# Expert weights of the second mixture: through a DRAM tensor and GpSimd in place of TensorE and VectorE

## The chip, the cores and the metric

The kernel runs on one core of a Trainium2 chip. The metric is the device time of one execution in microseconds, as the median of several runs. All work on the engines is in fp32. The profile names the engines PE (TensorE; PEld is its loading of weights), DVE (VectorE), ACT (ScalarE), POOL (GpSimd) and SP (SyncE, which here issues nearly all transfers).

## The reference, cut to what matters

Four layers follow one another on 64 sequences of 128 tokens with 128 features, each with a layer norm ahead of it and a residual sum behind it: cross-attention, a mixture of 8 gated experts (2 per token), a second cross-attention, and a second mixture. The change lies in the second mixture and in the preparation of the second attention, which runs at the same time.

```python
def _L1_xattn_ref(queries, keys, values, ...):      # keys = values = ctx: 120 rows, 16 heads of 8
    scores = jnp.einsum('bhqd,bhkd->bhqk', Q, K) / jnp.sqrt(d)
    attn = jax.nn.softmax(scores, axis=-1)
    out = jnp.einsum('bhqk,bhkd->bhqd', attn, V)
    return out @ W_o.T + b_o

def _L1_ffn_ref(x, Wg, bg, W1, W2):                 # E = 8, K = 2, R = 64, SCALING = 2
    logits = xf @ Wg.T + bg
    top_gates, top_idx = jax.lax.top_k(logits, K)
    top_gates = jax.nn.softmax(top_gates, axis=-1)
    h = jax.nn.gelu(jnp.einsum('nd,erd->enr', xf, W1), approximate=False)
    eout = SCALING * jnp.einsum('enr,edr->ned', h, W2)
    sel = jnp.take_along_axis(eout, top_idx[:, :, None], axis=1)
    out = jnp.sum(top_gates[:, :, None] * sel, axis=1)

x = x + _L1_xattn_ref(_layernorm(x), ctx, ctx, ...)
x = x + _L1_ffn_ref(_layernorm(x), ...)
```

The kernel computes the second mixture densely: the hidden rows of all 8 experts (8 x 64 = 512) are made for every token, each row is multiplied by the weight that its expert has for the token (zero for the six that were not chosen), and one product over all 512 rows gives the output. These weights are called shares or gates below.

## The kernel before, in words

The 64 sequences are worked on in 16 groups of four (GB = 4, NG = 16). The residual stream of each group stays in on-chip memory (`x_0` to `x_15`). The first attention, with the routing of the first mixture beside it, fills the first 620 us of the profiled execution, the tiles of the first mixture's experts follow, and the second attention with the second mixture beside it begins at about 955 us.

The order of the instructions on PE, DVE, ACT and POOL is the order in which the program writes them (`manual_schedule`). On SP a planner sets the order, by when it expects a transfer's inputs to be there. Each engine works through its queue in order, so an instruction that waits holds all that stand behind it.

`attention(1, ...)` is a loop over `it` from 0 to 68. Iteration `it` works on several sequences at different stages: the row maxima of the scores of sequence `it` (L407 on PE, L414 on DVE), the shift of sequence `it-1` by its maxima (L459 on PE, L462 on DVE, into the queries that the next iteration's scores read), scores and exponentials of `it-2` (L430 on PE, L438 on ACT), values of `it-3` (L475 on PE, L484 on ACT), and the output of `it-3` to `it-5` (L491 to L516). Eight PSUM banks are handed out in turn by `mtile()`.

With j = `it % 4`, `prep(it, half)` makes ready the next group of four, in two halves per iteration:

- j = 0: nothing.
- j = 1: the keys (L202 on PE, L207 on ACT), then `prep_heads`: four copies of the keys on DVE, each masked to a part of the heads (L313). The copies are first read by L407 in the next group's j = 0.
- j = 2: the values (L214 on PE, L221 on DVE), then the transposed normed input (L176 on PE, L177 on ACT).
- j = 3: the queries (L292 on PE, L295 and L301 on ACT).

Beside the attention runs `Aside1`. Once per iteration, after values and scores and ahead of the first half of `prep`, `piece` takes one step of the generator `experts()`. A group has four steps, and the first falls on j = 2:

1. j = 2: the gates of the group are transposed on PE (L1417) and copied by ACT into `gT` (L1419): row 32 j + e holds expert e's share for the 128 tokens of sequence j. Four products with `lw1` (L1424) give the hidden rows of two experts each for all 512 tokens, and ACT applies Gelu (L1427) into `h1`, chunk by chunk.
2. j = 3: 16 products of `gT` with the constant `select` (L1434; fp32 products take two instructions each) spread the shares over the partitions of their experts, into four PSUM banks, and DVE multiplies `h1` by them (L1439).
3. j = 0: the output product of two sequences over the four chunks (L1445), and its sum into the residual stream (L1450).
4. j = 1: the same for the other two, and the transfer of the group's result to memory (L1452).

`h1` and `gT` have one buffer each. In the same iterations POOL gathers the rows of the first mixture for later sequences (L1364), adds them to the residual stream (L1376), after which DVE takes the statistics of the sum (L112, L113), and makes the normed rows (L155 to L167, L526). `self.router.call` advances the routing of the second mixture (small instructions between L681 and L778, L1402, L1403), two calls per iteration.

The first group's experts begin in iteration 18 and those of the group numbered 12 in iteration 66. When the loop ends, four groups of the mixture are not finished, and `rest` takes the remaining steps of `experts()` one after the other, with three router calls after each.

A transfer in this kernel is one `dma_start` on SP, and its pieces are spread over the core's DMA engines.

## Time and profile before

| What | Value |
|---|---|
| median of 3 runs | 1576.28 us (1573.33 to 1578.66) |
| the profiled execution | 1516.1 us |
| its span, from the first to the last instruction | 1514.3 us |
| mean granted clock of TensorE | 0.989 |
| busy: PE, DVE, ACT, POOL | 94%, 73%, 56%, 42% of the span |
| first and last start of L1417 (gates transposed) | 1070.5 and 1500.4 us |
| L1417 of group 12, the last one inside the loop | 1461.4 us |
| L1417 of groups 13, 14 and 15 | 1479.6, 1491.1 and 1500.4 us |
| POOL busy from 1160 to 1190 us | 18.3 of 30 us |
| DMA share and rate from 1160 to 1190 us | 0.13, 36 GB/s |

The durations in the text below come from this one profiled execution. A group row of the profile gives the engine, the operation, the tile written and the tiles read, the shapes, the number of instructions, then the busy time in all, the mean of one in ns, and the idle time of the engine just ahead of such instructions with what ended it. The chain is followed back from the last instruction to what released each, and is shown in order of time (start, length, what). A timeline row has start, length, engine, line, and in brackets the idle time ahead. A clock of 1.00 is TensorE's full speed.

### The profile page before, as it was taken

Reading aid. Unit: us, or ns where it says so; the run is one execution under the profiler, and the core shown is the slowest. Engines: PE = TensorE matmul, PEld = TensorE weight load, DVE = VectorE, ACT = ScalarE, POOL = GpSimd, SP = SyncE. Lnnn points to the kernel's source line nnn. Section 1 sums busy time; section 2 is a strip of 40 time slices with the busy share of each in tenths; the row PEclk is TensorE's granted clock in tenths of the full one; section 3 lists DMA queues with packets and bytes.
Section 4 is the critical chain, followed back from the end, with each engine's and each line's share of the span. In section 5 each row is a group of like instructions: output and inputs, shape, how many; then the busy total and the mean of one; then the engine's idle time right before and its main releaser. Section 6 shows DMA issues by size and latency. Waiting matters only on the chain.

```text
span 1514.3 us, 42033 instructions
## 1 busy us (share of the span) xinstructions
PE 1421.0 (94%) x16620; PEld 1107.5 (73%) x16620; DVE 1102.4 (73%) x3024; ACT 847.6 (56%) x1740; POOL 640.4 (42%) x1195
## 2 busy tenths in 40 slices
PE   7999999999999999888999999898999999999987
PEld 5777777777777677777888888566666776767665
DVE  6777888888888988455754444687777778787763
ACT  4666666666666666543333333566667566666643
POOL 4123254646465635654001122377546555454210
PEclk9999999999999999999999999899999999999999
DMA  8433333333222221366766667111011111100000
GB/s 201 120 80 80 79 82 96 89 93 94 63 66 60 58 73 40 107 184 202 214 197 199 201 195 205 49 34 34 22 36 29 39 35 32 31 29 23 8 16 22
DMA packets 143719, 133.03 MB, mean 88 GB/s; under 512 B 48546, under 2 KB 126114, under 8 KB 141602
## 3 DMA queue, kind: packets, MB, share of 16 engines
q1 hardware_dynamic: 135330, 113.02, 27.3%
q0 software_dynamic: 8192, 17.32, 3.7%
q8 instruction: 132, 2.16, 0.6%
q14 instruction: 65, 0.53, 0.1%
HBM read 97.32 MB, written 32.97 MB: 86 GB/s over the span
## 4 chain that ended last, share of the span: by engine, by line
PE 69%; DVE 15%; DMA 4%; POOL 4%; ACT 4%; issue 2%; SPq 1%; POOLq 0%; DVEq 0%; ACTq 0%
PE bank L430 11%; PE bank L394 10%; PE bank L475 9%; PE bank L1115 9%; PE bank L1424 4%; PE bank L1445 4%; DVE nm L414 4%; PE bank L1128 3%; DMA q<-xs 2%; PE bank L407 2%; PE bank L214 2%; DVE q L462 2%; PE bank L511 2%; PE bank L681 2%; PE bank L202 2%
## 5 line engine op out<-in xcount | busy, mean ns | idle before, releaser
L414 DVE TENSOR_REDUCE nm<-bank 128x2 f32<-128x496 f32 (+1 forms) x768 | 463.5, 662 | 77.6 <-PE bank L430 61.8
L438 ACT ACTIVATE p<-bank 120x512 f32<-120x512 f32 (+1 forms) x768 | 402.1, 605 | 126.8 <-PE bank L430 123.9
L430 PE MATMUL bank<-q,k 32*120 32x256 f32 (+1 forms) x3072 | 438.1, 399 | 11.4 <-DVE nm L414 5.2
L430 PEld LDWEIGHTS bank<-q,k 32*120 32x120 f32 (+1 forms) x3072 | 293.5, 181 | 56.8 <-DVE nm L414 17.3
L394 PE MATMUL bank<-k,q 32*128 32x248 f32 x2048 | 291.0, 399 | 0.7 <-ACT q L334 0.5
L394 PEld LDWEIGHTS bank<-k,q 32*128 32x128 f32 x2048 | 202.2, 189 | 47.9 <-issue 11.0
L1120 DVE TENSOR_TENSOR p<-p,bank 128x256 f32<-128x256 f32 x213 | 88.0, 420 | 121.0 <-ACT p L1119 120.5
L475 PE MATMUL bank<-p,v 128*32 128x128 f32 (+1 forms) x4096 | 175.6, 275 | 0.2
L407 PE MATMUL bank<-k,qf 32*128 32x480 f32 x512 | 153.8, 602 | 0.8 <-ACT qf L295 0.8
L807 POOL DMA_INDIRECT xs<-xn,at x128 | 129.2, 1009 | 27.9 <-issue 24.3
L1119 ACT ACTIVATE p<-bank 128x256 f32<-128x256 f32 x213 | 81.0, 384 | 98.9 <-PE bank L1115 97.9
L484 ACT COPY ov<-bank 128x256 f32<-128x256 f32 x128 | 48.1, 376 | 143.5 <-PE bank L475 143.4
L475 PEld LDWEIGHTS bank<-p,v 128*32 128x32 f32 (+1 forms) x4096 | 108.8, 109 | 22.8 <-issue 13.7
L1364 POOL DMA_INDIRECT yb<-ys,back x112 | 108.5, 969 | 27.7 <-issue 19.5
L1115 PE MATMUL bank<-q 128*128 128x256 f32 x516 | 118.6, 379 | 1.6 <-ACT q L1106 1.6
L462 DVE SCALAR_TENSOR_TENSOR q<-bank,c_smask,q 128x256 f32<-128x256 f32 x256 | 111.1, 475 | 8.2 <-PE bank L459 7.8
L167 POOL TENSOR_SCALAR xn<-x,mv,rstd 128x128 f32<-128x128 f32 x252 | 110.2, 449 | 7.5 <-issue 1.4
L1115 PEld LDWEIGHTS bank<-q 128*128 128x128 f32 x516 | 94.7, 190 | 13.0 <-ACT q L1106 1.9
L475 PE MATMUL bank<-p,vc 120*32 120x128 f32 x2048 | 103.2, 272 | 0.0
L155 POOL TENSOR_SCALAR rstd<-mv 128x4 f32<-128x4 f32 x32 | 6.3, 198 | 219.9 <-DVE mv L113 123.0
L301 ACT ACTIVATE q<-bank,c_a_bq,c_hmask 128x512 f32<-128x512 f32 x124 | 90.1, 789 | 9.8 <-PE bank L292 9.8
L1157 POOL DMA_INDIRECT kvT<-ys,back x16 | 15.4, 961 | 189.7 <-DMA vc<-xs 114.0
(224 smaller groups left out, 2465.7 us busy)
## 6 DMA issues: line engine op xcount, KB each, us to landing
q<-in_w SPq DMA_DIRECT2D x43, 576.0 KB
vc<-in_w SPq DMA_DIRECT2D x28, 576.0 KB
vc<-in_ctx_v SPq DMA_DIRECT2D x16, 960.0 KB
ys<-zero SPq DMA_DIRECT2D x71, 128.0 KB
k<-in_ctx_k SPq DMA_DIRECT2D x32, 240.0 KB
q<-xs SPq DMA_DIRECT2D x43, 128.0 KB
ys<-q SPq DMA_DIRECT2D x43, 128.0 KB
x<-in_x SPq DMA_DIRECT2D x16, 256.0 KB
```

Source lines behind the costliest of these rows:

```text
L167: nc.gpsimd.tensor_scalar(xn[:, j, :D], xg[g][:, j, :], self.mv[:, b, 0:1], self.rstd[:, b : b + 1], ALU.add, ALU.mult,)
L301: nc.scalar.activation(q4s[g][:, :, s, :], pq.rearrange("p (b q) -> p b q", b=GB), AF.Identity, bias=w["bq"][:, s : s + 1], scale=hmask[:, ...
L394: nc.tensor.matmul(pa[:, u, :], lhsT=q4s[g][r, j, s, :], rhs=k2[g % 2][r, s // 2, j, :], start=True, stop=True,)
L407: lambda: nc.tensor.matmul(pa, lhsT=qfs[g][r, j, :], rhs=k4s[g][r, :, j, :], start=True, stop=True),
L414: nc.vector.tensor_reduce(nm[b % 2].rearrange("q i (a s) -> q a i s", s=16)[:, 2 * ra + v : 2 * ra + v + len(slots) // 2, :, 0], pa.rearra ...
L430: nc.tensor.matmul(pb[:n, v * 256 : (v + 1) * 256], lhsT=k2[g % 2][r, v, j, k0 : k0 + n], rhs=q4s[g][r, j, 2 * v : 2 * v + 2, :].rearrange ...
L438: nc.scalar.activation(ps_[b][:n, c, ra, :], pb[:n], AF.Exp, scale=SCALE)
L462: nc.vector.scalar_tensor_tensor(q, pm, smask[:, v : v + 1], q, ALU.mult, ALU.add)
L475: nc.tensor.matmul(pav[32 * ra : 32 * ra + 32, v * S : (v + 1) * S], lhsT=vs[g % 2][c][:, j, 4 * v + ra, i, :], rhs=p[:n, c, ra, (2 * v + ...
L807: s = nc.gpsimd.indirect_dma_start(xs, bass.IndirectOffsetOnAxis(at[:, j, k : k + 1], 0), xn, None)
L1115: nc.tensor.matmul(ph[:, u, :], lhsT=w[:, c, u * 128 : (u + 1) * 128], rhs=xT, start=True, stop=True)
L1364: nc.gpsimd.indirect_dma_start(y[:, k, b % 2, :], None, ys, bass.IndirectOffsetOnAxis(back[:, b, k : k + 1], 0),)
```

## The change

- The shares no longer go over PE. `gT` becomes a part of a larger tile `share` (128 x 4 x 512, 8 KB on each partition, one buffer). Four transfers write its rows, 8 x 128 each, to a DRAM tensor of 16 KB (two of these are used in turn). Two further transfers read it back, each into 64 partitions and with the same rows for all of them, in pieces of 2 KB: 1 MB a group in all. `select` and the 16 products are gone.
- The multiplication of `h1` by the shares moves from DVE (L1439, four instructions by sequence) to POOL (four by chunk). Its step comes two iterations after the hidden layer: an empty step stands between.
- Both output products and both sums are one step, in the iteration after the multiplication. A group has four steps as before: hidden layer in j = 2, nothing in j = 3, multiplication in j = 0, output in j = 1.
- After the Gelu of a group ACT carries out one Exp on a single element (`again`).
- `prep_heads` moves from the second half of j = 1 to j = 2, ahead of the values. This concerns the groups from the third on.

On SP the planner puts the four writes of a group after the copy of its gates, then the load of a later group's context (`kvT`), then the two reads, then the output.

```diff
                     elif g < NG:
                         pieces = (
-                            (), (lambda: prep_k(g), lambda: prep_heads(g)),
-                            (lambda: prep_v(g), lambda: prep_x(g)),
+                            (), (lambda: prep_k(g),),
+                            (lambda: (prep_heads(g), prep_v(g)), lambda: prep_x(g)),
                             (lambda: prep_q(g, 0), lambda: prep_q(g, 1)),
                         )[j]
...
     ys = hbm.tile([NTL * TT, D], F32, name="ys", tag="ys")
+    shares_ = [hbm.tile([E, GB, S], F32, name=f"shares_{k}", tag=f"shares_{k}") for k in range(2)]
...
-    select = load_const("select", [128, 4, 128], a["select"])
+    again = const.tile([1, 2], F32, name="again", tag="again")
+    nc.vector.memset(again, 0.0)
...
                 nc.tensor.transpose(pt, gates.rearrange("p b e -> p (b e)"), ident)
-                gT = self.pool.tile([128, S], F32, name="gT", tag="gT", bufs=1)
+                share = self.pool.tile([128, 4, GB * S], F32, name="share", tag="share", bufs=1)
+                gT = share[:, 3, :S]
                 nc.scalar.copy(gT, pt)
+
+                there = shares_[g % 2]
+                for j in range(GB):
+                    nc.sync.dma_start(there[:, j, :], gT[32 * j : 32 * j + E, :])
+                for i in range(2):
+                    nc.sync.dma_start(
+                        share[64 * i : 64 * i + 64],
+                        there.rearrange("(c i) j t -> i c (j t)", i=2)[i]
+                        .unsqueeze(0).to_broadcast([64, 4, GB * S]),
+                    )
                 xnT = self.xnTs.pop(g)
                 hT = self.pool.tile([128, 4, GB * S], F32, name="h1", tag="h1", bufs=1)
                 for c in range(4):
...
                     nc.scalar.activation(hT[:, c, :], ph, AF.Gelu)
+
+                nc.scalar.activation(again[:, 1:2], again[:, 0:1], AF.Exp)
                 yield
 
-                pg = [self.mtile().rearrange("p (c t) -> p c t", c=4) for _ in range(GB)]
+                yield
                 for c in range(4):
-                    for j in range(GB):
-                        r = slice(32 * j, 32 * j + 32)
-                        nc.tensor.matmul(
-                            pg[j][:, c, :], lhsT=select[r, c, :], rhs=gT[r, :], start=True, stop=True
-                        )
-                for j in range(GB):
-                    h = hT[:, :, j * S : (j + 1) * S]
-                    nc.vector.tensor_tensor(h, h, pg[j], ALU.mult)
+                    nc.gpsimd.tensor_tensor(
+                        hT[:, c, :], hT[:, c, :], share[:, c, :], ALU.mult
+                    )
                 yield
                 for j0 in range(0, GB, 2):
...
                             out[g * GB : (g + 1) * GB].rearrange("b p d -> p b d"), xg[g]
                         )
-                    yield
+                yield
```

The host no longer makes `select`.

More of the change, by code (lines that the diff above doesn't have):

```diff
@@ L1534, in _laid_out @@
     o["steps256"] = np.arange(CAP // TT, dtype=np.float32) * TT
-    t = np.zeros((4, 32, 4, 2, 64), np.float32)
-    for e in range(E):
-        t[:, e, e // 2, e % 2, :] = 1.0
-    o["select"] = t.reshape(128, 4, 128)
     o["tiles"] = np.arange(NA, dtype=np.float32).reshape(1, -1)
```

## The prediction

> **What bounds the kernel now.** I read the busy shares first, then the chain of work that ended last, the groups of instructions of the stretch the change touches (1066 us to the end), its timeline engine by engine, and the clock of the last 40 us. Every touched line runs after 1066 us, except the removed load of `select` at the start.
>
> ```profile
> PE 1421.0 (94%) x16620; PEld 1107.5 (73%) x16620; DVE 1102.4 (73%) x3024; ACT 847.6 (56%) x1740; POOL 640.4 (42%) x1195
> ```
> PE looks like the bound. In the stage itself the chain shows a mixture: PE in the heavy iterations, DVE and a table load in the light ones.
>
> ```profile
> 1311.33 1.28 ACT L438
> 1313.27 1.02 PE bank L1434 x24
> 1314.34 2.48 DVE h L1439 x4
> ...
> 1320.87 2.07 PE bank L1445 x16
> ...
> 1331.78 1.52 DVE k L313 x4
> ...
> 1495.97 0.70 DVE h L1439
> 1496.71 3.84 PE bank L1445 x32
> 1500.66 3.44 PE bank L1424 x8
> ```
> The first five lines lie in the loop: the table load before the exponentials, the share products, DVE's multiplication and the scaled keys end a wait once per group. The last three lie behind the loop, where one group's experts follow the other with nothing beside them.
>
> The groups of the stage, and the one POOL instruction of the shape that is added (in columns: busy, mean ns | idle before):
>
> ```profile
> L1439 DVE TENSOR_TENSOR h<-h,bank 128x512 f32<-128x512 f32 x64 | 39.7, 682 | 22.4 <-PE bank L1434 22.3
> L1434 PE MATMUL bank<-gT,c_select 32*128 32x128 f32 x512 | 30.2, 288 | 5.6 <-ACT p L438 4.7
> L526 POOL TENSOR_TENSOR x<-x,c_a_bo 128x512 f32<-128x512 f32 x11 | 14.0, 1269 | 0.9
> ```
>
> Where cover lies in an iteration, from the timeline of one group (brackets: idle before the instruction, and what ended it):
>
> ```profile
> 1240.59 0.76 DVE L221 TENSOR_TENSOR v<-bank,c_a_bv 120x256 f32<-120x256 f32 x2 [3.54 <-PE bank L214]
> 1244.87 1.28 ACT L438 ACT_TABLE_LOAD   x1 [0.76 <-PE bank L430]
> 1259.64 0.20 POOL L155 TENSOR_SCALAR rstd<-mv 128x4 f32<-128x4 f32 x1 [7.11 <-DVE mv L113]
> ```
> DVE stands 3.54 us while PE makes the hidden layer; POOL stands 7.11 us; ACT loads the table only when the first exponential is due. The last line is for later, a load of 256 KB from the chain's start, with 0.43 us of issue before it:
>
> ```profile
> 2.72 2.89 DMA kvT<-in_fsideT
> ```
>
> **The loop, part by part.** The experts' first step (L1417) starts at 1070.5 us for group 0 and 1461.4 us for group 12: 12 periods of 32.6 us on average, the full ones alternately 32.0 and 34.5. By the starts of L475 the four iterations last 7.2, 7.4, 8.3 and 11.5 us (j = 3, 0, 1, 2), in the lighter group 7.2, 7.0, 6.9 and 11.0. PE's own work per group, from the same rows without waits: 4 x (1.01 values + 1.94 scores + 0.87 outputs) + 3.9 hidden layer + 3.8 output product + 4.5 preparation = 27.5, and 1.3 of share products.
>
> *Removed, on PE and DVE (j = 3).* The share products: 1.2 us of PE and about 0.4 waiting for banks. DVE's 2.48 us, which stand before the shift of the next iteration (L462), on which the next scores wait. Nothing replaces them on either engine.
> *Heads moved.* L313, 1.5 us of DVE, leaves the second output product's iteration, where the next scores wait for it, for j = 2, into the 3.54 us of idle time before L221; without that cover it would cost its 1.5 us again. The keys it reads are made in j = 1 and the copies first used in j = 0.
> *Table load.* The small Exp behind the Gelu moves 1.28 us into ACT's idle time before L177 (1.46 us, and 0.39 before L506); that time bought 0.4 us on PE at most. The instruction itself is some 0.2 us (L741, 0.23).
> *Both output products together (j = 1).* Same PE and DVE work; j = 0 and 3 become light, and there DVE decides.
>
> Walking a group by these rows: j = 2 takes 10.3 (1.0 + 2.1 + 0.3 + 3.8 + 0.9 + 0.55 + 0.8 + 0.5 + 0.3), j = 3 4.9. DVE needs 4.95 per iteration (4 maxima 2.35, shift 0.87, 0.28, statistics 0.9, 0.55) and up to 0.9 for the router, so it holds PE at L491 and L430: j = 0 takes 4.3 to 4.8, j = 1 9.3 to 10.4 (0.6 to 1.1 of waiting for L462, then 3.8 in one block). Sum 28.8 in the lighter and 30.4 in the fuller group, 29.6 on average against 33.2: 3.6 saved.
>
> *Against it: POOL and DMAs.* The four multiplications cost 4 x 1.27 = 5.1 us per group on POOL. They come after four gathers and ahead of two additions (L1376) and two gathers. The additions are what DVE's statistics L112 wait for. POOL runs ahead: it did these additions at 1248.6 and DVE asked for the result at 1259.4. The new multiplication takes 5.1 of this 9 us lead and the shorter iterations some 4 more, so it is just enough; I charge 0.4 us a group. Here a rule speaks against the change. The Trainium skill (GPSIMD Engine Reference, 4.1 Engine selection) wants two-input elementwise work on VectorE, GpSimd being about 2 times slower. The rows have the same ratio, 1.27 to 0.68, and by the rule the loop would lose 4 x 0.59 = 2.4 us a group. By the rows of the loop it loses nothing there, since POOL has gaps of 7 us and DVE's time ends waits; I follow the rows in the loop and the rule behind it.
> Six DMA issues at about 0.4 us join SP's queue per group. Behind them stand the load of the next context (ordered between the writes and the reads, and waiting for L214) and the output. SP spends its time waiting, and neither is due for an iteration or more. The 1 MB of shares: writes issued 1.6, landed 2.05 after the last issue (the 256 KB load took 3.0 from issue, less 0.95 for its bytes at 280 GB/s; a busy DMA share of 0.7 moves 200 GB/s in the middle of the run), then 2.05 + 3.75 for the reads. With the context load ahead of the reads they land 12 us after L1417, when POOL ends its gathers; two iterations hide it. If the reads ran at half that rate (both ends: 3 to 7.5 us), 3 us would fall on POOL, C would wait about 2 a group.
>
> So 3.2 saved per full group, 11 of them; 1.8 in the last period, where light iterations leave only 16 us before C and the shares need 17; 1 before group 0 (four moved heads). Sum -38; with 2 allowed for waits of PE that I could not place, **-36** (-24 to -53: the lower end with 2 us a group for POOL or DMA, the upper where DVE never holds PE).
>
> **Behind the loop.** Groups 12 to 15. The tail's clock, in stretches of 3 us (start:end, length, busy of PE, PEld, DVE, ACT, POOL, then the clock):
>
> ```profile
> 1472.00:1475.00 3.00, 0.45 (x5) 0.26 (x3) 2.25 (x13) 0.43 (x1) 1.41 (x3) 1.00 0.00 0
> 1475.00:1478.00 3.00, 1.44 (x5) 0.67 (x5) 1.07 (x6) 1.64 (x3) 1.74 (x4) 0.84 0.30 87
> 1478.00:1481.00 3.00, 3.00 (x11) 2.48 (x12) 1.03 (x6) 0.27 (x1) 0.00 (x0) 0.50 0.00 0
> 1481.00:1484.00 3.00, 3.00 (x4) 1.06 (x4) 0.30 (x2) 2.14 (x3) 0.00 (x0) 0.52 0.00 0
> ```
> One gap of 3.1 us on PE (1472.4 to 1475.6), and PE runs at half clock until 1484.
>
> Before, a group takes 9.3 us here (1491.0 to 1500.4): hidden layer 3.6, shares 1.2, multiplication 0.7 until the first output product, product 3.8. There is one `h1` and one `share`, and PE's queue has the next group's L1417 behind this group's product, so in the changed kernel nothing overlaps: transposition and copy 0.75; writes 1.25 to the last issue + 2.05; reads 2.05 + 3.75 and 0.5 of waits and issues (bounds 3.0 and 7.5 for the 3.75); multiplication 5.2, all four before the first product, since it sums over c; product. The hidden layer and Gelu end at 6 to 8 us and are hidden. So the product begins 15.6 us after L1417, PE having stood for 8 to 10 us. At half clock it takes 7.5 instead of 3.8 (L681 took 1.87 for 0.96). The skill (TensorE: Matmul & The Clock Gate, Part 1) has an idle window of about 3.4 us before the clock halves and 3.4 us of work to restore it: then 5.5. In the rows the half clock lasted 6 us of unbroken work (1477.9 to 1484): then 7.5. By the page the product loses 1.7 each, by the row 3.7; nearer the row, I take 6.6. Period 22.3 (19 to 26), plus 0.3 for an output issue between the share writes in groups 14 and 15.
> From L1417 of group 13 the kernel ended after 34.7 us; now 3 x 22.3 + 0.6 + 4.8 (last addition and store, as before) = 72.3: +37.6. From group 12 to 13: 18.3 now; then 15.6 + 6.6 + transposition, copy and logits of group 15 2.8 = 25.0: +6.7. Together **+44** (+32 to +55).
>
> **Sum.** 1516.1 - 36 + 44 = 1524. The profiled execution lies 60.2 below the median; where that time is the trace can't show, so I add the difference unscaled (scaled by 1.04 it changes by 0.3): 1576.3 + 8 = **1584.5**, 0.5% slower. About 0.3% (4.7 us) is what this measurement can tell from no change.
>
> **Rivals.**
> *Freed down to PE's work (faster).* Place: j = 0 and 1. For: DVE, busy 78% from 1066 to 1430 us or 26 us a group, has 23.5 left of 29.6, and maxima may be taken late as long as banks are free. Against: each L430 needs the L462 before it. Price: groups at 28.3, 4.9 saved x 11 = 54, and the tail's 44 in return: 1567. It decides from a period below about 28.8, where the loop's gain passes the tail's cost by 4.7.
> *POOL paces.* Additions late for L112, or C waiting for the fourth multiplication. For: POOL's lead shrinks from 9 us to nearly nothing. Against: 54% of a group busy now, 17.7 us, with the 5.1 22.8 of 29.6. Price: some 1.6 to 2 a group, 11 x 1.8 = 20 more: 1604.
> *No effect to be seen.* Loop and tail cancel, with the clock restored early (tail 37) and the loop at 3.2: 1577.
>
> **Chances and range.** Forecast 0.48 (its own range 1580 to 1597); freed 0.24; POOL paces 0.16; cancel 0.12. Slower: 0.46 and 0.16, 0.62. Faster: 0.22 of the freed case. The same: 0.12, and 0.02 each from the forecast's and the freed case's edges, 0.16. Range 1564 to 1604: it holds the freed case but its far end, and half of POOL's.
>
> **What would show it.** Right: L1417 of groups 1 to 10 every 29 to 31 us; L313 under L1424; ACT's table load before L506; PE idle some 8 us ahead of each of the last four output products, clock near 0.5 in them, last L1417s 22 us apart. Wrong: DVE's L112 or PE's product waiting for POOL inside the loop (loop too dear), or shares landing much sooner than 10 us after L1417 in the tail, or full clock there (tail too dear in my sum).

## The result, and the profile after

The changed kernel takes 1603.26 us (median of 4 runs, 1599.78 to 1606.11), the kernel before 1577.47 us in the runs beside it: a ratio of 1.0164, with a 95% interval of 1.0141 to 1.0188. That is 25.8 us slower, where 8 were predicted.

The time of the unchanged kernel differs between sessions on the chip (1577 here, 1574 and 1567 in two of the sets of experiments below, 1520 in the other two, and the 1516.1 us of the profile before belong by their time to the latter), so a ratio always refers to the runs of before in the same set, and traces are subtracted only between kernels of the two sets at 1520.

The busy shares and the groups of the changed stage, from the page of the profile after (groups: busy, mean ns of one | idle before, and what ended it):

```profile
PE 1441.6 (90%) x16108; PEld 1112.3 (70%) x16108; DVE 1097.1 (69%) x2961; ACT 852.0 (53%) x1759; POOL 722.2 (45%) x1259
...
L1447 POOL TENSOR_TENSOR h<-h,share 128x512 f32<-128x512 f32 x64 | 79.1, 1268 | 114.7 <-DMA share<-shares 107.4
...
L1455 PE MATMUL bank<-c_lw2T,h 128*128 128x128 f32 x512 | 75.9, 310 | 39.7 <-POOL h L1447 36.9
```

PE carries out 512 instructions fewer and is less busy as a share, so the time went into waiting. POOL's multiplication costs 1.27 us each, as taken from L526. It waited 107.4 us for shares, and PE waited 36.9 us for it. Those 36.9 us lie behind the loop. The chain of work that ended last shows a period there, from group 12's writes to its product (start, length, what):

```profile
1511.53 1.22 DMA shares<-share
1512.93 0.58 SPq L1428
1513.51 0.05 issue
1513.56 6.74 DMA share<-shares
1520.36 0.10 issue
1520.46 4.93 POOL h L1447 x4
1525.39 0.04 issue
1525.44 4.87 PE bank L1455 x26
```

Write, read, multiplication and product follow one another with nothing between, as the prediction had them. The gates were transposed at 1509.74 us.

Inside the loop the masked keys and the table load lie where the change put them. From the timeline of a group (brackets: idle before):

```profile
1276.55 1.76 DVE L313 TENSOR_SCALAR k<-k,c_hmask 128x480 f32<-128x480 f32 x4
1280.13 1.28 ACT L1442 ACT_TABLE_LOAD   x1
1280.17 0.76 DVE L221 TENSOR_TENSOR v<-bank,c_a_bv 120x256 f32<-120x256 f32 x2 [1.87 <-PE bank L214]
```

The 3.54 us of DVE's idle time before L221 have shrunk to 1.87, and L313 stands in the rest. The same timeline, 10 us later, shows what was not foreseen:

```profile
1290.60 4.93 POOL L1447 TENSOR_TENSOR h<-h,share 128x512 f32<-128x512 f32 x4 [2.23 <-DMA share<-shares]
...
1291.37 0.59 DVE L718 TENSOR_TENSOR eq<-lg,m 128x64 f32<-128x64 f32 x1
...
1291.99 1.19 DVE L719 TENSOR_TENSOR eq<-eq,order 128x64 f32<-128x64 f32 x1
...
1293.47 0.93 DVE L723 TENSOR_TENSOR one<-order,at 128x64 f32<-128x64 f32 x1
...
1295.02 0.33 PE L504 MATMUL bank<-ident,o 128*128 128x128 f32 x1 [2.13 <-DVE nm L414]
```

The multiplication begins 15.5 us after the transposition (1275.05), not 12, and beside it three small instructions of the router on DVE take 0.59, 1.19 and 0.93 us; elsewhere they take about 0.2. Each of them ends just behind one of the four multiplications. PE then waits 2.13 us for the maxima that stand behind them.

The starts of the gates' transposition give the periods. In this profile, groups 0 to 12 take 410.7 us and the kernel ends 90.0 us after group 12's start. In the profile of before these were 390.8 and 53.0. The second pair can be compared across sets: in every trace with the old tail, in all the sets, it lies between 52.5 and 53.7. The first can't, and so the loop was studied by experiments.

### The profile page after: what moved, and what is told of

It reads as the page before. It is cut to its first block, busy times and chain, and to the rows that moved or that the text cites. A ratio compares the mean times of both kernels' runs of the same rounds, so it can differ in the third digit from the quotient of the medians.

```text
span 1599.7 us, 41266 instructions
## 1 busy us (share of the span) xinstructions
PE 1441.6 (90%) x16108; PEld 1112.3 (70%) x16108; DVE 1097.1 (69%) x2961; ACT 852.0 (53%) x1759; POOL 722.2 (45%) x1259
## 4 chain that ended last, share of the span: by engine, by line
PE 68%; DVE 14%; DMA 7%; issue 3%; POOL 3%; ACT 2%; SPq 1%; another core or an unknown queue 0%; POOLq 0%; ACTq 0%; DVEq 0%
PE bank L430 12%; PE bank L394 9%; PE bank L475 9%; PE bank L1116 9%; DVE nm L414 5%; PE bank L1455 4%; PE bank L1129 3%; DMA q<-xs 3%; PE bank L1437 3%; PE bank L407 3%; PE bank L511 2%; PE bank L214 2%; PE bank L292 2%; DVE q L462 2%; PE bank L202 2%
## 5 line engine op out<-in xcount | busy, mean ns | idle before, releaser
L414 DVE TENSOR_REDUCE nm<-bank 128x2 f32<-128x496 f32 (+1 forms) x768 | 465.3, 663 | 107.6 <-PE bank L430 76.0
L430 PE MATMUL bank<-q,k 32*120 32x256 f32 (+1 forms) x3072 | 457.8, 404 | 28.6 <-issue 9.1
L430 PEld LDWEIGHTS bank<-q,k 32*120 32x120 f32 (+1 forms) x3072 | 301.8, 183 | 80.1 <-issue 18.3
L475 PE MATMUL bank<-p,v 128*32 128x128 f32 (+1 forms) x4096 | 185.7, 281 | 4.8 <-issue 3.9
L407 PE MATMUL bank<-k,qf 32*128 32x480 f32 x512 | 147.9, 616 | 2.2 <-ACT qf L295 0.8
L475 PEld LDWEIGHTS bank<-p,v 128*32 128x32 f32 (+1 forms) x4096 | 113.8, 111 | 33.2 <-issue 21.6
L1447 POOL TENSOR_TENSOR h<-h,share 128x512 f32<-128x512 f32 x64 | 79.1, 1268 | 114.7 <-DMA share<-shares 107.4
L1116 PE MATMUL bank<-q 128*128 128x256 f32 x516 | 124.8, 394 | 3.0 <-ACT oT L506 3.0
L1455 PE MATMUL bank<-c_lw2T,h 128*128 128x128 f32 x512 | 75.9, 310 | 39.7 <-POOL h L1447 36.9
L1116 PEld LDWEIGHTS bank<-q 128*128 128x128 f32 x516 | 98.9, 198 | 16.3 <-ACT oT L506 3.4
L475 PE MATMUL bank<-p,vc 120*32 120x128 f32 x2048 | 104.2, 272 | 0.7 <-issue 0.7
L1455 PEld LDWEIGHTS bank<-c_lw2T,h 128*128 128x128 f32 x512 | 69.5, 218 | 50.4 <-POOL h L1447 43.1
```

The lines of the kernel that those rows point to most:

```text
L407: lambda: nc.tensor.matmul(pa, lhsT=qfs[g][r, j, :], rhs=k4s[g][r, :, j, :], start=True, stop=True),
L414: nc.vector.tensor_reduce(nm[b % 2].rearrange("q i (a s) -> q a i s", s=16)[:, 2 * ra + v : 2 * ra + v + len(slots) // 2, :, 0], pa.rearra ...
L430: nc.tensor.matmul(pb[:n, v * 256 : (v + 1) * 256], lhsT=k2[g % 2][r, v, j, k0 : k0 + n], rhs=q4s[g][r, j, 2 * v : 2 * v + 2, :].rearrange ...
L475: nc.tensor.matmul(pav[32 * ra : 32 * ra + 32, v * S : (v + 1) * S], lhsT=vs[g % 2][c][:, j, 4 * v + ra, i, :], rhs=p[:n, c, ra, (2 * v + ...
L1116: nc.tensor.matmul(ph[:, u, :], lhsT=w[:, c, u * 128 : (u + 1) * 128], rhs=xT, start=True, stop=True)
L1455: nc.tensor.matmul(po[:, j, :], lhsT=hT[:, c, (j0 + j) * S : (j0 + j + 1) * S], rhs=lw2[:, c, :], start=(c == 0), stop=(c == 3),)
```

## The experiments

### First set: where the loop's gain went (before: 1520.36 us)

Theory: the walk of the prediction (28.8 and 30.4 us a group) is right, and something of POOL's multiplication or of the transfer gives the gain back. Rivals: the walk itself was wrong; or only the tail costs. The unchanged kernel, measured against itself, gave 1.0004 (0.9987 to 1.0022).

> The kernel before, unchanged, for a second profile. Its first profile (1516.1 us) lies 61 us below its timed runs (1577), the changed kernel's first profile (1601.5) only 2 below its own. If the first profile was an unusually quick execution, this one comes out near 1575, and the places where it is longer than the first (gates of group 0 transposed at 1070.5, of group 12 at 1461.4 us) tell what the profiles can be compared for. If quick executions are usual for this kernel under the profiler, it comes out near 1516 again. In the first case the untouched 1070 us and the loop's 391 us share the 60 us; the tail of 53 us should stay within 1.

Its profile took 1518.0 us, near 1516 as in the second case, and all its runs in this set lie between 1517.8 and 1530.1.

*Small reads.* The tile `share` is filled once with 0.25, and 64 KB instead of 1 MB are read back.

```diff
-                        share[64 * i : 64 * i + 64],
-                        there.rearrange("(c i) j t -> i c (j t)", i=2)[i]
-                        .unsqueeze(0).to_broadcast([64, 4, GB * S]),
+                        share[64 * i : 64 * i + 16, 0:1],
+                        there.rearrange("(c i) j t -> i c (j t)", i=2)[i, 0:1]
+                        .unsqueeze(0).to_broadcast([16, 1, GB * S]),
```

> The changed kernel with the reads of the shares cut from 1 MB to 64 KB a group (16 partitions and one chunk of each half; the rest of the tile holds 0.25, so the products are not the reference's). All steps, waits and POOL's multiplications stay. Theory T (the 1 MB transfer holds PE up in the loop, by the stops of about 2.2 us that have no releaser in the profile, and lengthens the tail): those stops go, the loop's 410 us from group 0 to 12 fall by 15 to 30, the tail's 90 us fall by 4 x 4 to 5 = 16 to 20; in all 1555 to 1570. Theory P (POOL's multiplication holds DVE): the loop stays within 5 us of 410 and only the tail falls; about 1585.

*No multiplication.* POOL's four instructions are left out; all transfers stay.

```diff
-                for c in range(4):
-                    nc.gpsimd.tensor_tensor(
-                        hT[:, c, :], hT[:, c, :], share[:, c, :], ALU.mult
-                    )
```

> The changed kernel without POOL's multiplications (the Gelu's rows go unweighted into the output product, so the output is not the reference's). The transfers stay in full, but nothing waits for them. Theory P: DVE's small instructions beside the multiplication (L719 took 1.19 us in place of 0.23) are short again and the loop falls by 15 to 25 from 410. Theory T: the stops of 2.2 us stay and the loop falls by less than 8. By both the tail loses its wait for transfer and multiplication, 4 x 12 = 48 of its 90 us less what the hidden layer takes by itself: about 45 left, so 1555 by T and 1535 by P.

*Old tail.* Groups 12 to 15 take the old way: shares by PE, multiplication on DVE, and the two output products in separate steps.

```diff
-                for j in range(GB):
+                for j in range(GB if g < NEW else 0):
                     nc.sync.dma_start(there[:, j, :], gT[32 * j : 32 * j + E, :])
...
+                else:
+                    pg = [self.mtile().rearrange("p (c t) -> p c t", c=4) for _ in range(GB)]
...
+                    for j in range(GB):
+                        h = hT[:, :, j * S : (j + 1) * S]
+                        nc.vector.tensor_tensor(h, h, pg[j], ALU.mult)
```

> The changed kernel with groups 12 to 15 in the old way (shares by 16 products, multiplication on DVE, two output steps; the constant is loaded into the free part of the share tile ahead of group 12). The loop up to group 12 is the changed one. If the tail behind the loop is the changed kernel's loss as summed in the prediction, its 90 us return to 53 and the time falls by 37 to 1566. If the loop is the loss and the tail only moves waits about, it falls by less than 20. What is then left against the kernel before (1577) is the loop alone.

Measured, in us; the last column is from the transposition of group 12 to the end, and the row before is the unchanged kernel of the same set. Lighter and fuller are typical periods of the groups that alternate:

| Kernel | Ratio (95%) | Lighter, fuller | Groups 0 to 12 | Group 12 to end |
|---|---|---|---|---|
| before | 1 | 31.9, 34.5 | 390.8 | 53.7 |
| no multiplication | 0.9676 (0.9653 to 0.9699) | 28.8, 31.0 | 353.3 | 49.2 |
| small reads | 0.9998 (0.9986 to 1.0011) | 28.8, 36.1 | 378.3 | 70.1 |
| old tail | 0.9971 (0.9956 to 0.9987) | 31 to 33, 34 to 36 | 394.1 | 52.6 |

Without the multiplication the loop is what was walked, 37.5 us shorter than before, although the 1 MB a group is still read. So neither the walk nor the transfer by itself is at fault. With the multiplication and small reads 25.0 us come back, nearly all in the fuller groups. With the full reads 15.8 more come back, and the loop has gained nothing: the old tail is 0.3% below before by the timed runs, and its span is 2.7 us above by the traces. The expectations were written for before at 1577, so only differences can be set beside them: theory T had 15 to 30 us in the loop for the small reads, and 15.8 came; theory P had 15 to 25 for leaving the multiplication out, and 40.8 came. Each has a part.

The fuller groups have the router's instructions in j = 0. The timeline of one, with small reads:

```profile
1115.37 4.92 POOL L1449 TENSOR_TENSOR h<-h,share 128x512 f32<-128x512 f32 x4
1116.01 4.44 DVE L718 TENSOR_TENSOR eq<-lg,m 128x64 f32<-128x64 f32 x1
1120.49 0.63 DVE L719 TENSOR_TENSOR eq<-eq,order 128x64 f32<-128x64 f32 x1
1121.84 2.34 DVE L414 TENSOR_REDUCE nm<-bank 128x4 f32<-128x480 f32 x4
...
1122.54 0.47 PE L504 MATMUL bank<-ident,o 128*128 128x128 f32 x1 [4.21 <-DVE nm L414]
```

and the same instruction without the multiplication:

```profile
1118.04 0.19 DVE L718 TENSOR_TENSOR eq<-lg,m 128x64 f32<-128x64 f32 x1
1118.27 0.22 DVE L719 TENSOR_TENSOR eq<-eq,order 128x64 f32<-128x64 f32 x1
```

L718 takes 4.44 us instead of 0.19, and ends 0.16 us after POOL's four multiplications (1120.29). PE stands for 4.21 us for the maxima behind it. The fuller group is 5.1 us longer (36.1 to 31.0), and summed over the periods of groups 0 to 12 the difference is the 25.0 us. What the stop of 4.21 us leaves of the 5.1 is PE's clock: it is 0.50 from 1124 to 1127 us, and L475 takes 1.94 us there instead of 1.14.

With the full reads (old tail), which is the loop of the changed kernel, the picture is another. A lighter group:

```profile
1143.07 1.78 SPq L1433 DMA_DIRECT2D share<-shares  x2
...
1152.52 4.96 POOL L1453 TENSOR_TENSOR h<-h,share 128x512 f32<-128x512 f32 x4 [2.98 <-ACT q L302]
...
1157.43 1.53 POOL L1380 TENSOR_TENSOR x<-x,yb 128x256 f32<-128x256 f32 x2
1159.00 0.29 DVE L113 BATCH_NORM_STATS2 st<-x 128x6 f32<-128x128 f32 x1 [2.85 <-POOL x L1380]
...
1160.19 5.44 PE L1472 MATMUL bank<-c_lw2T,h 128*128 128x128 f32 x32 [2.58 <-DVE nm L415]
```

The multiplication starts 15.1 us after the transposition (1137.37), behind a wait of 2.98 us. The two additions behind it end at 1158.96, DVE's statistics have waited 2.85 us for them, and PE's product waits 2.58 us for the maxima behind the statistics; the product itself takes 5.44 us instead of 3.84 us after that stop, since the clock is 0.52 from 1161 to 1164 us. (The line names ACT as what ended POOL's wait, though ACT's work there has nothing to do with the multiplication; in six of the ten groups from 1100 to 1430 us the view of the waits names the reads of shares, and in the group shown the DMA share falls from 0.98 in the microsecond from 1150 to 0.02 in the one from 1152, where the multiplication begins.) A fuller group of the same kernel:

```profile
1119.57 4.95 POOL L1453 TENSOR_TENSOR h<-h,share 128x512 f32<-128x512 f32 x4 [2.81 <-ACT p L439]
...
1121.06 1.06 DVE L733 TENSOR_SCALAR cap<-one 128x64 f32<-128x64 f32 x1
...
1122.15 1.22 DVE L735 TENSOR_TENSOR rest<-lg,cap 128x64 f32<-128x64 f32 x1
```

Here the multiplication is so late that L719 (the L718 of the other kernels) has run before it, in 0.19 us. It holds L733 and L735 instead, each to the end of one multiplication (0.19 and 0.23 us without it). PE's longest waits of this kernel from 1110 to 1400 us (in total, times, longest):

```profile
PE bank L1472 <- DVE nm L415: 14.4, 8, 2.8
PE bank L431 <- DVE q L463: 6.2, 5, 1.6
```

The first is the product behind the late statistics; in the fuller group shown, the shift L463 of the second stands behind the held instructions. Against no multiplication the first four lighter groups lose 2.5 to 4.5 us and the first four fuller ones 2.9 to 4.7: here the loss is as large where POOL holds nothing on DVE as where it does.

How long PE is busy from group 0 to 12 shows a second cost of every stop. Without the multiplication, with small reads and with full reads (start:end, length, busy of PE, PEld, DVE, ACT, POOL, then clock, DMA share and rate):

```profile
1075.00:1428.00 353.00, 337.44 (x3780) 251.29 (x3784) 284.15 (x853) 245.68 (x488) 192.13 (x286) 1.00 0.29 67
1073.00:1451.00 378.00, 346.05 (x3780) 257.28 (x3784) 309.00 (x853) 246.16 (x488) 251.11 (x334) 0.96 0.12 31
1072.00:1466.00 394.00, 357.19 (x3788) 266.00 (x3792) 299.23 (x854) 246.35 (x488) 251.25 (x334) 0.95 0.27 60
```

For nearly the same instructions PE is busy 8.6 us longer with small reads and 19.8 us longer with full reads. Its clock falls to half behind the stops; so about a third of the 25.0 us and half of the 40.8 us are PE working more slowly, and the rest is PE standing.

### Second set: the change alone again, and its other parts (before: 1573.67 us)

*The changed kernel, unedited.*

> The changed kernel once more, so that it stands beside the same runs of the kernel before as the others. From the parts: loop as in the kernel with the old tail (394 us from group 0's L1417 to group 12's, so no gain over 391), tail some 37 us longer than in it: 1517 + 37 = 1554, against 1520 before, ratio 1.022. If PE's stops of 2 us without a releaser, seen in the first profile of the change, belong to the change and not to that session, they come again and the loop takes 405 or more: 1565 or more.

It measured 1597.30 us, 1.0152 (1.0115 to 1.0189). The 1554 of the expectation were meant for before at 1520; its ratio, 1.022, was too high. Groups 0 to 12 take 409.7 us, the rest 89.8. PE's stops of 2.2 us are there again, but they also stand in the next kernel, masked keys and Exp alone, which has no transfer of shares. The waits of PE from 1110 to 1400 us there (us in total, times, longest):

```profile
PE bank L430 <- ACT ov L484: 8.8, 4, 2.2
...
PE bank L459 <- DVE h L1442: 3.5, 4, 1.4
PE bank L430 <- issue: 2.2, 1, 2.2
```

So these stops, which no trace of the sets at 1520 us has, come with the set and not with the change. What causes them stays open.

*Masked keys and Exp alone.* The kernel before, with `prep_heads` in j = 2 and the small Exp; no other part of the change.

```diff
-                            (), (lambda: prep_k(g), lambda: prep_heads(g)),
-                            (lambda: prep_v(g), lambda: prep_x(g)),
+                            (), (lambda: prep_k(g),),
+                            (lambda: (prep_heads(g), prep_v(g)), lambda: prep_x(g)),
...
+                nc.scalar.activation(again[:, 1:2], again[:, 0:1], AF.Exp)
```

> The kernel before with two edits of the change alone: the masked keys (L313) made in j = 2 ahead of the values, and the small Exp behind the Gelu. Shares stay on PE, the multiplication on DVE, the tail as before. By the prediction's steps 1.5 us for the heads and 0.4 for the table, 1.9 a group, 11 groups: 21 us less, 1500. Rival: the idle time before L221 is only there because of other waits, and 2.48 us of DVE's multiplication in j = 3 still holds the scores: under 5 us, 1515 to 1520.

*The same, and both output products in one iteration.*

```diff
                     nc.vector.tensor_tensor(h, h, pg[j], ALU.mult)
                 yield
+                yield
...
-                    yield
+                yield
```

> As the last, and both output products in one iteration (j = 1) with an empty step in j = 0. If light and heavy iterations are better apart, as in the walk of the prediction, it gains another 1 us a group in the loop, and loses 3 to 6 us behind it, where group 12's products now fall: 1495. Rival: PE's long block in j = 1 holds the scores as it did, and only the loss behind the loop is left: 1505.

The first measured 0.9957 (0.9945 to 0.9970): 6.8 us, or 0.6 a group instead of 1.9. It is faster than both kernels, but lies nearer to the rival; the second wait above is a part of that, since PE's L459 still waits for DVE's multiplication in j = 3. The second measured 0.9989 (0.9978 to 1.0001): putting the products together gave 5 us back rather than gaining. By the walk its advantage needs light iterations, and these exist only once the shares and the multiplication are off PE and DVE; in the kernel without multiplication, where they are, the walked periods came out.

*Scalings on POOL.* Small reads, and four scalings of one operand instead of the multiplications.

```diff
-                    nc.gpsimd.tensor_tensor(
-                        hT[:, c, :], hT[:, c, :], share[:, c, :], ALU.mult
+                    nc.gpsimd.tensor_scalar(
+                        hT[:, c, :], hT[:, c, :], 0.5, 0.5, ALU.mult, ALU.mult
```

> The small reads of before (64 KB instead of 1 MB a group, the rest of the tile 0.25), and POOL's four multiplications h times share replaced by four scalings of h by a constant: of about the same length, but with one operand from memory instead of two. The output is not the reference's. Theory 'two operands on POOL hold two operands on DVE': L718 beside them takes 0.2 us and not 4.4, fuller groups take 31 us and not 36, the kernel about 25 us less than with small reads alone (1521), so 1496 to 1500. Rival 'POOL's time itself is late for something': fuller groups stay near 36 us and the time near 1520. Rival 'any POOL work on memory slows DVE's': in between, L718 stretched though less.

It measured 0.9788 (0.9753 to 0.9824), groups alternating 33.7 and 34.3 us, with PE's stops in them: the surplus of the fuller groups is gone. But one scaling takes 0.63 us and not 1.27, and in the trace L718 came only after the four, so this run doesn't say whether the number of operands matters.

### Third set: operands, lateness, and DVE (before: 1520.16 us)

*Eight scalings*, so that POOL is busy as long as with the multiplications.

```diff
-                for c in range(4):
+                for c in (0, 1, 2, 3) * 2:
                     nc.gpsimd.tensor_scalar(
```

> As the scaling on POOL with small reads, but with eight scalings of h by a constant instead of four, so that POOL is busy for about 5 us (8 x 0.63), as with the four multiplications, and L718 falls beside them. The output is not the reference's. Theory 'two operands on POOL hold two operands on DVE': L718 stays at 0.2 to 0.4 us, fuller groups about as long as lighter ones but for 2 us, ratio as with four scalings (0.979) or up to 0.005 more. Rival 'any POOL work on the same memory holds it': L718 takes 4 us again, fuller groups 5 us longer than lighter ones, ratio near 1.00.

*Multiplication of h by h*: two operands, all transfers, but no wait for shares.

```diff
-                        hT[:, c, :], hT[:, c, :], share[:, c, :], ALU.mult
+                        hT[:, c, :], hT[:, c, :], hT[:, c, :], ALU.mult
```

> The changed kernel with all its transfers, but POOL multiplies h by h, so that its multiplications have two operands and their length and wait for no transfer of shares (the shares are not applied, the output is not the reference's). It is set beside the small reads, which had the loop at 378 us, and the old tail, 394 us. If shares that land late cost those 16 us, the loop is as with small reads: lighter groups near 28.8, fuller near 36, ratio near 1.00 or a little below, as the tail waits for no shares either. If the 1 MB transfer itself slows the engines or the gathers, the loop stays some 16 us longer, ratio near 1.01. In both, L718 takes some 4 us where it falls beside the multiplication.

*DVE multiplies from memory*, in j = 0, with the old tail.

```diff
-                        nc.gpsimd.tensor_tensor(
+                        nc.vector.tensor_tensor(
                             hT[:, c, :], hT[:, c, :], share[:, c, :], ALU.mult
```

> The changed kernel with the old tail (groups 12 to 15 in the old way), and in the loop the multiplication in j = 0 on DVE in place of POOL, from the same two tiles in memory; the 1 MB of shares still goes through memory. Theory 'POOL's multiplication takes the gain': without any multiplication groups took 28.8 and 31.0 us; DVE's own four cost at most 4 x 0.7 = 2.8 a group where DVE decides, so 31 to 33 us on average, loop 353 + 11 x (0 to 2.8) = 353 to 384 us and a ratio to the kernel before of 0.975 to 0.995. Rival 'the transfer itself slows the loop': no better than with POOL (0.997).

| Kernel | Ratio (95%) | Lighter, fuller | Groups 0 to 12 | Group 12 to end |
|---|---|---|---|---|
| eight scalings | 0.9811 (0.9779 to 0.9843) | 28.8, 32.6 (once 36.2) | 365.1 | 56.8 |
| h by h | 0.9841 (0.9806 to 0.9876) | 28.8, 35.1 | 373.1 | 52.7 |
| DVE multiplies | 0.9938 (0.9921 to 0.9956) | 30.8 to 33.3, 33.9 to 34.6 | 387.3 | 53.3 |

The eight scalings refute both theories as they were put. Two groups of that kernel in the timeline:

```profile
1108.83 4.70 POOL L1449 TENSOR_SCALAR h<-h 128x512 f32<-128x512 f32 x8
1109.47 0.67 DVE L718 TENSOR_TENSOR eq<-lg,m 128x64 f32<-128x64 f32 x1
...
1170.91 4.10 POOL L1449 TENSOR_SCALAR h<-h 128x512 f32<-128x512 f32 x7
1170.95 4.21 DVE L718 TENSOR_TENSOR eq<-lg,m 128x64 f32<-128x64 f32 x1
```

POOL's one-operand instructions hold L718 too: mostly for about the length of one (0.67 us beside 0.6), and in one group until the whole row of them has ended (4.21). That group is the one of 36.2 us, where the other fuller groups among the first eight took 32.6 and 32.7: within one trace the full hold costs some 3.5 us. It is not the number of operands on POOL that decides whether DVE is held. What differs is whether DVE gets in between two of POOL's instructions. With the small reads and with h by h, L718 was held to the end of the row in all four fuller groups of the first eight; with the scalings it mostly got in; and in the changed kernel DVE got in behind each multiplication, with the same instructions on POOL (0.59, 1.19 and 0.93 us above). On DVE's side two operands aren't needed either: L733, which reads one tile, took 1.06 us in place of 0.19 beside a multiplication. The maxima (L414), which read a PSUM bank, kept their 0.65 us each beside it.

The Trainium skill (SBUF — State Buffer, Who interferes with whom) has a rule that fits: a DVE instruction with two inputs from SBUF contends with a GpSimd instruction that reads SBUF, over a shared pair of ports, which is an exclusive lock. Of DVE's two-port modes it says that whoever issues first has the pair for the whole instruction and the other is fully blocked. The runs agree that DVE is blocked and not merely slowed, and some go further: with the small reads four instructions in a row kept DVE out for all four (4.44 us), not for the rest of one (at most 1.27).

With h by h, L718 took 3.48 to 3.56 us beside multiplications of 4.03 in all, as expected. The loop is 5.2 us shorter than with small reads, about what multiplications shorter by 0.9 us give in the fuller groups (35.1 against 36.1). So with every transfer in place, and only the wait for the shares gone, the 15.8 us that the old tail's loop had on top are gone: they are the lateness of the shares and not the load on memory. The lighter groups, with 28.8 us, lose nothing at all.

DVE's own multiplication is the third way. The loop is 3.5 us shorter than before, at 387 just beyond the dearer end of the expectation (384), and better than with POOL (394). DVE's 2.48 us, which stood in j = 3 before, are now in the light j = 0, again ahead of the shift on which the next scores wait:

```profile
1184.99 2.48 DVE L1453 TENSOR_TENSOR h<-h,share 128x512 f32<-128x512 f32 x4
...
1188.50 0.87 DVE L463 SCALAR_TENSOR_TENSOR q<-bank,c_smask,q 128x256 f32<-128x256 f32 x2
...
1189.03 0.47 PE L431 MATMUL bank<-q,k 32*120 32x256 f32 x1 [1.88 <-DVE q L463]
```

### A fourth set: DVE's multiplication behind the shift (before: 1567.21 us)

```diff
-                    for c in range(4):
-                        nc.vector.tensor_tensor(
-                            hT[:, c, :], hT[:, c, :], share[:, c, :], ALU.mult
-                        )
+                    self.late = (hT, share)
...
         def call(self, it, mtile):
             self.router.call(None, mtile)
+            self.calls += 1
+            if self.late and self.calls % 2 == 0:
+                hT, share = self.late
+                self.late = None
+                for c in range(4):
+                    nc.vector.tensor_tensor(
+                        hT[:, c, :], hT[:, c, :], share[:, c, :], ALU.mult
+                    )
```

> As with DVE's multiplication from memory and the old tail, but the four multiplications stand at the end of iteration j = 0, behind the shift (L463 there) instead of ahead of it. Where they stood, PE's scores of j = 1 waited 1.9 to 2.6 us for the shift, 15.5 us over nine groups. Theory 'in a light iteration DVE ahead of the shift is the bound': these waits go, the maxima of j = 1 come 2.5 us later instead and cost PE about 1 us for banks, so 1 us a group less: loop 377 and a ratio of 0.987. Rival 'DVE's 2.5 us cost the same wherever they stand in j = 0': 0.994 again.

It measured 1549.68 us, 0.9887 (0.9864 to 0.9909): 1.1% below before, and so faster than both kernels, with the old tail behind the loop. The wait for the shift is gone from PE's list (15.5 us with the multiplication ahead of it), and a smaller one took its place:

```profile
PE bank L431 <- issue: 7.0, 4, 2.2
PE bank L1469 <- DVE h L1492: 3.4, 5, 1.2
```

The loop of 377 that was expected can't be checked, since PE's stops are there too (the first of the two lines) and the loop took 398.3 us with them. The ratio is as expected, but whether moving the multiplication gave the 0.5% between 0.9938 and 0.9887 is not shown: the two were measured in different sets, and in a set with PE's stops the changed kernel's ratio, too, came out 0.7% lower (1.0152) than its parts gave without them (1.022).

## Why the prediction was right or wrong

The direction was right and the time, 1603.3, lies at the upper edge of its range (1604). The likeliest case wasn't what happened: 17.8 of the 25.8 us were not in its sum. That the range holds the time is in part luck, since two errors ran against each other: the loop was to gain 36 us and all but the tail gained some 11, and the tail was to cost 44 and cost 37.

*What bounds, and the walk of a group: right.* 28.8 and 30.4 were walked; with POOL's multiplication left out the trace has 28.8 and 31.0, and groups 0 to 12 are 37.5 us shorter, against the 36 to 38 of the sum. PE's and DVE's parts, the light and heavy iterations and their order, were read rightly from the trace of before.

*Heads and table load: hidden as said, but not worth their sum alone.* L313 lies under the hidden layer; its mean went from 463 to 639 ns in the loop, beside POOL, and idle time of DVE still covered it. The table load stands under ACT's idle time. Done alone, the two gave 0.6 us a group and not 1.9: it seems that a gain of that kind counts only together with the edit that makes the same iterations light, since the whole sum came out without the multiplication.

*"POOL and DMAs … it is just enough; I charge 0.4 us a group": the step that failed.* The runs at 1520 us show 40.8 us over groups 0 to 12 instead of some 5, by two paths and a term that was put at nothing.
The first path the step had, and priced too low. The shares were to land 12 us after L1417; the multiplication began 15.1 us or more after it in the groups shown. Reads and context load took 9.5 us from the issue of the first read to the multiplication in the group shown, where 2.05 + 3.75 were summed. Behind the late multiplication stand the additions, DVE's statistics, the maxima and PE's product. In the loop of the changed kernel this is the larger path: 14.4 us of PE's waits against 6.2, and the lighter groups, where POOL holds nothing on DVE, lose as much as the fuller ones. Without the wait for shares (h by h) they lose nothing. The prediction's own bound ("half that rate … C would wait about 2 a group") was this path.
The second path the step didn't have: it weighed POOL's 5.1 us as time of POOL alone, as if DVE ran freely beside it. Where the shares are in time, DVE's small instructions are held through the whole multiplication, 4.44 us for 0.19, and the multiplication costs 25.0 us. Where they are late, as in the changed kernel, the multiplication meets other instructions or DVE gets in between, and less is held (0.59, 1.19 and 0.93 us, or 1.06 and 1.22). So 25.0 and 15.8 are the steps from kernel to kernel, and not the shares of the two paths in the changed one; what the hold alone costs there, no run measured.
The term put at nothing is PE's clock inside the loop: 19.8 of the 40.8 us are PE working longer on the same instructions, at half clock behind the stops.

*The rule against the change.* The rule "two-input elementwise work on VectorE" was set aside, because its ratio of durations (1.27 to 0.68) would not fall on the bound. It gave 2.4 us a group; measured were 3.4 (40.8 / 12). That the two are near each other proves nothing for its reason, slowness, and nothing against it: the additions stand behind the 4.96 us of the multiplication, and no run made it shorter with the shares late. The rule on the shared ports, told above, was to be weighed beside it. Multiplying on DVE was better than on POOL in the same place (387.3 to 394.1).

*The tail: right in mechanism, dearer by 7 in the sum.* From group 12 to the end it took 36 to 37 us longer (90.0 and 89.8, against 52.5 to 53.7), where 44 were summed. The start of the product, put at 15.6 us after the transposition, is right: POOL ended at 1525.39 and the transposition began at 1509.74, 15.65 us. The writes landed sooner than summed (1.22 us after the last issue, 2.05 taken), the reads later (6.74 in all). The term that was mis-sized is the product at half clock, 6.6; six of its 32 instructions also ran between the multiplications, where all were to come behind them. The stretches of 3 us of the changed kernel show it (start:end, length, busy of PE, PEld, DVE, ACT, POOL, then clock, DMA share and rate):

```profile
1514.00:1517.00 3.00, 1.72 (x14) 1.34 (x12) 2.12 (x10) 1.93 (x5) 0.00 (x0) 1.00 0.88 212
1517.00:1520.00 3.00, 0.00 (x0) 0.00 (x0) 2.60 (x15) 0.00 (x0) 0.00 (x0) 0.79 0.69 137
1520.00:1523.00 3.00, 0.80 (x3) 0.51 (x3) 0.11 (x1) 0.00 (x0) 2.54 (x3) 0.50 0.01 3
1523.00:1526.00 3.00, 2.15 (x6) 1.56 (x7) 0.00 (x0) 0.00 (x0) 2.83 (x4) 0.50 0.00 0
1526.00:1529.00 3.00, 3.00 (x16) 3.00 (x15) 0.42 (x1) 0.00 (x0) 2.70 (x6) 0.50 0.00 0
1529.00:1532.00 3.00, 2.08 (x19) 1.84 (x18) 1.23 (x8) 0.68 (x2) 0.00 (x0) 1.00 0.10 30
```

The clock falls to half in PE's stop, as said. Unbroken work began at 1525.44 us and the clock is full from 1529, after 3.6 us and not 6, and the product's last part took 4.87 us (5.34 in the next group). The 3.4 us of the skill's page (TensorE: Matmul & The Clock Gate, Part 1), from which 5.5 followed, were nearer here than the row that was preferred. Row and page don't exclude each other. In these traces the granted clock changes only in steps of 3.41 us (at 1477.06 and 1483.89 us before; at 1518.77 and 1529.01 us here, three steps apart), and it came back at the end of the first or second step that PE had filled. Work that begins just ahead of a step, as here, waits 3.6 us; work that begins within one, as in the trace of before (1477.88), waits 6.0. In one point the traces differ from the page: the clock does not need 3.4 us of idle time to fall. In the loop with full reads a stop of 2.58 us was enough (1157.6 to 1160.2 us, then 0.52 from 1161 to 1164). The periods were 22.8, 20.9 and 21.1 us instead of 25.0 and 22.3.
The other runs split the tail: 70.1 us with small reads, 52.7 where nothing waits for shares. Of the 37 us, about 20 are thus the megabyte's reading and 17 the round trip through memory with small reads. POOL's multiplication and the single step of the products cost nothing there on balance.

*The rivals.* "POOL paces", at 1604, came to the right figure and to half of the reason: the additions were late for the statistics, as it said. The other half, DVE held by POOL, was in no case. That the figure fits is luck too: its sum had the loop at a gain of 16 us and the tail at 44, for some 11 and 37. "Freed to PE's own work" fell: in no run did a group from 0 to 8 take less than 28.8 us.

*What stays open.* The tail costs 37 us and the whole kernel 25.8, so the rest of it gained some 11 us beside the runs of the result, and nothing much in the first set (0.9971 with the old tail). There is no trace of before from a set with PE's stops. The nearest is masked keys and Exp alone, whose loop took 417.4 us where the changed kernel's took 409.7 in the same set; without the stops these were 390.8 for before and 394.1. So at least a part of the 11 us lies in the loop, which loses less in the sets with stops than the old one. Why it does is not shown.

## What to carry to other kernels

Before work is moved to GpSimd because it has time to spare, look at what VectorE does in the same iterations: a VectorE instruction that reads SBUF may be held to the end of GpSimd's instruction, and in the worst case of its whole row, so price the move by what is behind that instruction, not by GpSimd's busy time. Price also what stands behind the moved work on GpSimd's own queue: here it was two additions that VectorE waited for. And price each stop of PE with the half clock that follows it. A transfer that is hidden in the loop is exposed behind it, where one group follows the other; there the old way, four groups long, is worth keeping. And a multiplication that must be on a busy engine goes behind the instruction that the next stage waits for: so placed, with the old tail, the kernel was 1.1% faster than before, the lowest ratio of those here that compute the reference's output.

## What the runs showed of the hardware that was not expected

- A DVE instruction of 0.19 us took 4.44 us beside four multiplications on POOL of 4.92 us in all, and ended 0.16 us after them. In the changed kernel it took 0.59 us beside the same four, and beside eight one-operand scalings about 0.67 us mostly and 4.21 once. What decides whether DVE gets in between two of POOL's instructions stays open.
- PE's clock was back to full 3.6 us after unbroken work began, where it took 6.0 us in the trace of before: it changes in steps of 3.41 us. A stop of 2.58 us of PE was enough to halve it.
- In some of the sets PE stops for 2.2 us at L430 with no releaser that fits, with and without the change, and the unchanged kernel takes 47 to 57 us longer.
